# Cross-attention on one core: key and output projections as fifteen 172-column block products instead of eleven matmuls of 256 columns, with partial sums kept in PSUM

## The chip, the core and the metric

One core of one Trainium2 chip. The metric is the device time of one execution in microseconds (us). The kernel before took 1415.97 us (median of two runs, 1415.4 and 1416.54).

## What is computed

For 64 batches, all in float32; x is 64 x 256 x 512 and ctx_768 is 64 x 256 x 384, the hidden width H is 512:

```python
text_p  = einsum('bld,dh->blh', x, W_text) + b_text          # queries
audio_p = einsum('bsd,dh->bsh', ctx_768, W_audio) + b_audio  # keys and values
Q, K, V = layer_norm(text_p, g1, beta1), layer_norm(audio_p, g2, beta2), audio_p
alpha   = softmax(einsum('blh,bsh->bls', Q, K) / sqrt(512))
H_hyper = einsum('bls,bsh->blh', alpha, V) @ W_out + b_out
return layer_norm(H_hyper + x, g_out, beta_out)
```

## The kernel before

The values are never formed. The attention weights multiply the raw context rows (z, 384 wide), and z is multiplied by W_audio @ W_out, folded once at the start (`fold_multiply`, L252), with a folded bias (`bao_sb`). Every batch has five products. In float32 each `nc.tensor.matmul` call becomes two MATMUL rows and two weight loads in the profile.

- **q** (512 x 512 weights): seven block products of a Strassen-Winograd scheme, 14 calls of 256 columns; **k** (384 x 512): seven block products, 11 calls; **y**, the output (384 x 512): 11 calls. All three are `Blocks` objects: `products` (L487) fills PSUM, two products to a bank, and `leave` (L499) adds each bank to SBUF rows with VectorE, five additions of 128 x 512 per object. The sums of the left-hand blocks are made by GpSimd (`sum_x`, `sum_c`), those of the weights once at the start.
- **scores** (L526): 8 calls; **z** (`context`, L592): 6 calls, copied out of PSUM by ScalarE (L599).

So a batch is 50 calls of 256 columns. Around them: ScalarE takes the square sums (L392), scales rows (`normalise`, L420), applies gamma and beta (`affine`, L458), does the exponentials (L543), their division (L557) and the output's two statistics (L617, L622). VectorE turns 32 x 32 squares (L91, L451), takes the maxima (L536), and shifts and settles the output (L729, L738). GpSimd makes the reciprocal roots (L353, L355) and adds x to the output (`add_x`, L608). Rows that must be transposed go through DRAM: `store` writes them, `fetch` reads them back as squares, with DMAs on the SyncE queue (SP).

The order is written out by hand: each engine executes its own instructions strictly in the order in which the Python code issues them, and the tile layer inserts the semaphore waits. PSUM is six rotating one-bank buffers (`p_pj`) and two more for scores and z (`p_at`). A round of the main loop works on three batches at once: the scores of batch b, q and k of batch b+2, z and y of batch b-1. On TensorE it stands as scores, q, z, k, y, and within q, k or y no product reads what `leave` made of an earlier one: `leave` only empties banks. The one result that TensorE needs back in the same round is z, whose sums GpSimd makes for y while k runs. 62 rounds run, then the last two batches are finished in a tail.

Of the kernel before, what the change touches and what calls it, by code (L numbers as in the profile page):

```python
# [22 lines left out]
def kernel(  # L23
# [18 lines left out]

# [7 lines left out]
    scale = 1.0 / math.sqrt(H)  # L72

    const = ctx.enter_context(tc.tile_pool(name="const", bufs=1))
    xin = ctx.enter_context(tc.tile_pool(name="xin", bufs=3))
    cin = ctx.enter_context(tc.tile_pool(name="cin", bufs=3))
    blk = ctx.enter_context(tc.tile_pool(name="blk", bufs=2))
    work = ctx.enter_context(tc.tile_pool(name="work", bufs=2))
    small = ctx.enter_context(tc.tile_pool(name="small", bufs=4))
    scratch = ctx.enter_context(tc.tile_pool(name="scratch", bufs=3, space=bass.MemoryType.DRAM))  # L80
    p_pj = ctx.enter_context(tc.tile_pool(name="p_pj", bufs=6, space=PSUM))
    p_at = ctx.enter_context(tc.tile_pool(name="p_at", bufs=2, space=PSUM))

# [49 lines left out]
    def row(v, name):  # L133
        t = const.tile([P, H], F32, tag=name, name=name)
        nc.sync.dma_start(t, v.rearrange("(o h) -> o h", o=1).broadcast_to([P, H]))
        return t
# [4 lines left out]

# [4 lines left out]
    wa_sb = const.tile([P, AC, H], F32, tag="wa", name="wa")  # L146
# [14 lines left out]
    ba_sb = row(b_audio, "ba")  # L161
# [32 lines left out]
    def keep_busy(n):  # L194

        ps = p_pj.tile([P, P], F32, tag="pj", name="ps_ones")
        for _ in range(n):
            nc.tensor.matmul(ps, lhsT=ones, rhs=ones, start=True, stop=True)

    class RowTurn:  # L200

# [31 lines left out]
    def bias_parts():  # L233

        part = work.tile([P, D], F32, tag="e", name="part")
        nc.vector.tensor_scalar(part, wo_sb[:, 0, :], bac_sb[:, 0:1], None, ALU.mult)
        for k in range(1, HC):
            nc.vector.scalar_tensor_tensor(
                part, wo_sb[:, k, :], bac_sb[:, k : k + 1], part, ALU.mult, ALU.add
            )  # L240

        nc.vector.tensor_tensor(part[:1], part[:1], bo_sb, ALU.add)
        return part

    wao_sb = const.tile([P, AC, D], F32, tag="wao", name="wao")
    ps_wao = {}

    def fold_multiply(a):

        ps = ps_wao[a] = p_pj.tile([P, D], F32, tag="pj", name="ps_wao")  # L250
        for k in range(HC):
            nc.tensor.matmul(  # L252
                ps,
                lhsT=waT[k][:, bass.ts(a, P)],
                rhs=wo_sb[:, k, :],
                start=(k == 0),
                stop=(k == HC - 1),
            )

    def fold_evict(a):  # L260
        nc.scalar.copy(wao_sb[:, a, :], ps_wao.pop(a))

    def fold_bias(part):

        ps = p_pj.tile([P, D], F32, tag="pj", name="ps_bao")
        nc.tensor.matmul(ps, lhsT=ones, rhs=part, start=True, stop=True)
        bao = const.tile([P, D], F32, tag="bao", name="bao")
        nc.vector.tensor_copy(bao, ps)
        return bao
# [21 lines left out]
    H2 = H // 2  # L291

    def weight_sums(w_sb, n, name, between=lambda: None):

# [28 lines left out]
    def sum_c(cT, tag="csum"):  # L326

        part = lambda i, j: cT[:, j, bass.ts(i, P)]
        s = work.tile([P, 5, P], F32, tag=tag, name=tag)
        add = nc.gpsimd.tensor_tensor  # L330
        add(s[:, 0], part(1, 0), part(1, 1), ALU.add)
        add(s[:, 1], s[:, 0], part(0, 0), ALU.subtract)
        add(s[:, 2:4], cT[:, 0:3:2, :P], cT[:, 0:3:2, P:], ALU.subtract)
        add(s[:, 4], part(0, 1), s[:, 1], ALU.subtract)
        return {
            1: [part(0, 0)], 2: [part(0, 1), part(0, 2)], 4: [part(1, 1), part(1, 2)],
            5: [s[:, 0], part(1, 2)], 6: [s[:, 1]], 7: [s[:, 2]], 3: [s[:, 4], s[:, 3]],
        }

    def weights_of_three(w_sb, name):  # L340

        ws = weight_sums(w_sb, 1, name)
        for n, k2 in ((2, 0), (3, 1), (5, 1), (4, 0)):
            ws[n].append(w_sb[:, 2, (1 - k2) * H2 : (2 - k2) * H2])
        return ws
# [12 lines left out]
    class Projection:  # L358


        def __init__(self, name, b, srcT, w_sb, bias, nch, nt):
            self.name, self.b, self.nt, self.nch = name, b, nt, nch
            self.srcT, self.w_sb, self.bias = srcT, w_sb, bias
            self.rows = work.tile([P, nt, H], F32, tag=f"{name}r", name=f"{name}r_{b}")
# [3 lines left out]
            self.ps = {}  # L368

        def multiply(self, t, chunks):  # L370
            if t not in self.ps:
                self.ps[t] = p_pj.tile([P, H], F32, tag="pj", name=f"ps_{self.name}")
# [9 lines left out]
        def evict(self, t):  # L382
            nc.vector.tensor_tensor(self.rows[:, t, :], self.ps.pop(t), self.bias, ALU.add)
# [57 lines left out]
        def turn(self):  # L441
            self.T = work.tile(
                [P, HC, self.nt * P], F32, tag=f"{self.name}T", name=f"{self.name}T_{self.b}"
            )
            if self.name == "q" or self.b >= B - 2:
                turn(self.T, self.sq, HC)
                return


            for t in range(self.nt):  # L450
# [15 lines left out]
    class Blocks(Projection):  # L466

        def __init__(self, name, b, sides, weights, bias):
            super().__init__(name, b, None, None, bias, None, 2)
            self.sides, self.weights, self.banks = sides, weights, {}

        def products(self, *ns):

            for n in ns:  # L480
                group = next(g for g in ((1, 6), (2, 5), (3, 4), (7,)) if n in g)
                if group not in self.banks:
                    self.banks[group] = p_pj.tile([P, 2, H2], F32, tag="pj", name=f"ps_{self.name}")
                place = self.banks[group][:, group.index(n), :]
                pairs = list(zip(self.sides[n], self.weights[n]))
                for i, (side, w) in enumerate(pairs):
                    nc.tensor.matmul(  # L487
                        place, lhsT=side, rhs=w, start=(i == 0), stop=(i == len(pairs) - 1)
                    )

        def leave(self, *ns):

            bank = self.banks[(1, 6) if ns[0] in (1, 6) else ns]
            quarters = self.rows.rearrange("p t (k h) -> p (t k) h", k=2)
            c1, c2 = quarters[:, :2], quarters[:, 2:]
            add = lambda o, i0, i1: nc.vector.tensor_tensor(o, i0, i1, ALU.add)  # L499
            if len(ns) == 1:  # L500
                j = int(ns[0] == 6)
                bank = bank[:, j : j + 1, :].broadcast_to([P, 2, H2])
            if ns == (1,):
                add(c1, bank, self.bias.rearrange("p (k h) -> p k h", k=2))
            elif ns == (6,):
                add(c2, bank, c1)
            elif ns == (2, 5):
                add(quarters[:, 1:3], bank, quarters[:, 1:3])
            elif ns == (3, 4):
                add(quarters[:, 0:4:3], bank, c2)  # L510
            elif ns == (7,):
                add(c2, bank, c2)

    class Attention:
        def __init__(self, b):
            self.b, self.qT, self.kT = b, q.pop(b).T, k.pop(b).T
            self.summed = ()

        def scores(self, end=False):
            if end:  # L520
                self.sc = p_pj.tile([P, LT, S], F32, tag="pj", name="ps_sc")
            else:
                self.sc = p_at.tile([P, LT, S], F32, tag="at", name="ps_sc")
            for t in range(LT):
                for k in range(HC):
                    nc.tensor.matmul(  # L526
                        self.sc[:, t, :],
                        lhsT=self.qT[:, k, bass.ts(t, P)],
                        rhs=self.kT[:, k, :],
                        start=(k == 0),  # L530
                        stop=(k == HC - 1),
                    )
# [5 lines left out]
        def exponentials(self):  # L538

            self.e = work.tile([P, LT, S], F32, tag="e", name=f"e_{self.b}")  # L540
# [30 lines left out]
        def transpose_e(self):  # L571
            self.ps_e = p_pj.tile([P, ST, L], F32, tag="pj", name="ps_e")
# [10 lines left out]
        def context(self):  # L583

            self.zT = work.tile([P, AC, L], F32, tag="zT", name="zT")
            self.ps_z = []
            for lo in range(0, AC, 2):
                n = min(2, AC - lo)
                ps = p_at.tile([P, 2, L], F32, tag="at", name="ps_z")
                for j in range(n):  # L590
                    for s in range(ST):
                        nc.tensor.matmul(  # L592
                            ps[:, j, :],
                            lhsT=c_rows[self.b][:, s, bass.ts(lo + j, P)],
                            rhs=self.eT[:, s, :],
                            start=(s == 0),
                            stop=(s == ST - 1),
                        )
                nc.scalar.copy(self.zT[:, lo : lo + n, :], ps[:, :n, :])  # L599

        def start_products(self):

            self.o = Blocks("y", self.b, sum_c(self.zT, "zsum"), wao_blocks, bao_sb)
            self.y = self.o.rows

        def add_x(self):
            for t in range(LT):
                nc.gpsimd.tensor_tensor(self.y[:, t, :], self.y[:, t, :], x_rows[self.b][:, t, :], ALU.add)  # L608
# [22 lines left out]
        def start_output(self):  # L631
            self.y = work.tile([P, LT, H], F32, tag="yr", name=f"y_{self.b}")
# [3 lines left out]
        def multiply(self, t):  # L636
# [458 lines left out]
```

## Time and profile before

| | us |
|---|---|
| median of two runs | 1415.97 |
| span of the profiled execution, first to last instruction | 1411.8 |
| what lies outside the span, against the median | 4.2 |
| start, up to the scores of round 0 | 43.0 |
| main loop, from there to the scores of the tail | 1330.7 |
| tail | 38.1 |
| one full round (scores to scores) | 21.58 |
| busy in a full round: TensorE, VectorE, ScalarE, GpSimd | 21.58, 19.1, 14.6, 13.5 |

The profiled execution's own time is not listed apart from its span; the span is taken as that execution and 4.2 us as what lies around it. In rows of the profile, PE is TensorE's matmul, PEld its weight load, DVE VectorE, ACT ScalarE, POOL GpSimd. "x4" in a timeline means four equal rows merged, and the time beside it runs from the first one's start to the last one's end. The recorded end of a matmul is later than the start of the next: rows overlap in the pipeline, so a matmul's price is read from start to start.

### The profile page before, as it was taken

To read this page: it belongs to the slowest core of one execution; us is meant where nothing else is said; L and a number is where in the kernel's file an instruction comes from. 1 tells how busy PE (TensorE), PEld (TensorE's weight loads), DVE (VectorE), ACT (ScalarE), POOL (GpSimd) and SP (SyncE) were. 2 spreads that over 40 slices of the span, in tenths; PEclk is the share of its full clock that TensorE was granted. 3 is DMA by queue.
4 is the path that set the end of the run, shared out by engine and by line. 5 is a ranking of instruction groups with operands and counts; after the bars stand their busy time and mean duration, and the time that the engine had idled before them with its cause. 6 is when DMAs were issued, how large, how long until landed. Compare 5 with 4: busy or idle time off the path is not lost.

```text
span 1411.8 us, 22761 instructions
## 1 busy us (share of the span) xinstructions
PE 1403.2 (99%) x6437; PEld 1220.4 (86%) x6437; DVE 1230.4 (87%) x1758; ACT 935.0 (66%) x2298; POOL 871.0 (62%) x1294
## 2 busy tenths in 40 slices
PE   9999999999999999999999999999999999999998
PEld 5888888888888888888888888888888888888885
DVE  6888898898888988988988889889889888898887
ACT  4667667676676676676766766766767667667663
POOL 5556666656656666666566566666665665666645
PEclk9999999999999999999999999999999999999999
DMA  8798877888888887787887887877888888878763
GB/s 211 206 259 229 245 233 218 246 232 224 241 243 219 232 233 228 234 226 237 231 230 235 225 238 232 231 232 232 221 243 237 222 240 239 222 235 232 223 212 125
DMA packets 450437, 322.32 MB, mean 228 GB/s; under 512 B 154885, under 2 KB 382981, under 8 KB 450310
## 3 DMA queue, kind: packets, MB, share of 16 engines
q1 hardware_dynamic: 450214, 320.72, 80.3%
q8 instruction: 52, 0.85, 0.3%
q14 instruction: 75, 0.61, 0.2%
q10 hardware_dynamic: 96, 0.13, 0.0%
HBM read 203.83 MB, written 116.92 MB: 227 GB/s over the span
## 4 chain that ended last, share of the span: by engine, by line
PE 98%; DVE 1%; POOL 1%; DMA 0%; ACT 0%; issue 0%; DVEq 0%; ACTq 0%
PE ps_q L487 27%; PE ps_k L487 21%; PE ps_y L487 20%; PE ps_sc L526 15%; PE ps_z L592 12%; PE ps_wao L252 1%; PE ps_y L639 1%; PE ps_q L374 0%; PE ps_k L374 0%; DMA c<-in_ctx_dram 0%; DVE yr L499 0%; PE ps_rows L214 0%; POOL yr L608 0%; POOL x L772 0%; DVE kr L499 0%; PE ps_wa L227 0%
## 5 line engine op out<-in xcount | busy, mean ns | idle before, releaser
L499 DVE TENSOR_TENSOR qr<-ps_q,qr 128x512 f32<-128x512 f32 x252 | 174.3, 692 | 88.9 <-PE ps_q L487 86.1
L526 PE MATMUL ps_sc<-kT,qT 128*128 128x256 f32 x1024 | 231.5, 379 | 0.0
L353 POOL TENSOR_SCALAR ve<-var 128x2 f32<-128x2 f32 x126 | 43.4, 344 | 290.0 <-ACT junk L392 289.8
L526 PEld LDWEIGHTS ps_sc<-kT,qT 128*128 128x128 f32 x1024 | 194.6, 190 | 26.9 <-issue 0.5
L543 ACT ACTIVATE e<-ps_sc,nmx 128x256 f32<-128x256 f32 x128 | 59.4, 468 | 230.3 <-DVE nmx L536 230.3
L608 POOL TENSOR_TENSOR yr<-yr,x 128x512 f32<-128x512 f32 x124 | 155.7, 1277 | 70.8 <-DVE yr L499 70.8
L499 DVE TENSOR_TENSOR kr<-ps_k,kr 128x512 f32<-128x512 f32 x252 | 174.4, 692 | 22.5 <-DVE kr L499 0.9
L487 PE MATMUL ps_q<-wtsum,xsum 128*128 128x256 f32 x756 | 193.7, 379 | 0.0
L499 DVE TENSOR_TENSOR yr<-ps_y,yr 128x512 f32<-128x512 f32 x248 | 171.6, 692 | 21.7 <-DVE yr L499 0.5
L487 PE MATMUL ps_k<-wa,cT 128*128 128x256 f32 x630 | 177.1, 379 | 0.0
L592 PE MATMUL ps_z<-eT,c 128*128 128x256 f32 x768 | 176.2, 379 | 0.0
L487 PE MATMUL ps_y<-wao,zT 128*128 128x256 f32 x620 | 174.1, 379 | 0.0
L355 POOL TENSOR_TENSOR rstd<-ve,nhalf 128x2 f32<-128x2 f32 x192 | 157.3, 819 | 16.0
L592 PEld LDWEIGHTS ps_z<-eT,c 128*128 128x128 f32 x768 | 145.9, 190 | 20.3 <-issue 0.5
L487 PEld LDWEIGHTS ps_q<-wtsum,xsum 128*128 128x128 f32 x756 | 143.6, 190 | 19.5
L458 ACT ACTIVATE qT<-qT,columns 128x256 f32<-128x256 f32 x256 | 133.0, 593 | 4.1 <-DVE qT L91 4.0
L458 ACT ACTIVATE kT<-kT,columns 128x256 f32<-128x256 f32 x256 | 132.2, 588 | 2.3 <-DVE kT L91 1.3
L487 PEld LDWEIGHTS ps_k<-wa,cT 128*128 128x128 f32 x630 | 119.6, 190 | 16.2
L487 PEld LDWEIGHTS ps_y<-wao,zT 128*128 128x128 f32 x620 | 117.7, 190 | 16.0
L420 ACT ACTIVATE kr<-kr,rstd 128x512 f32<-128x512 f32 x126 | 84.0, 714 | 71.6 <-POOL rstd L355 71.6
L392 ACT ACTIVATE junk<-kr 128x512 f32<-128x512 f32 x126 | 79.4, 630 | 77.9 <-DVE kr L499 73.5
L487 PE MATMUL ps_q<-wt,xT 128*128 128x256 f32 x504 | 129.0, 379 | 0.0
(160 smaller groups left out, 2976.3 us busy)
## 6 DMA issues: line engine op xcount, KB each, us to landing
kd<-kr SPq DMA_DIRECT2D x64, 512.0 KB, 3.1
kq<-kd SPq DMA_DIRECT2D x256, 128.0 KB, 3.4
qd<-qr SPq DMA_DIRECT2D x64, 512.0 KB, 4.8
qq<-qd SPq DMA_DIRECT2D x256, 128.0 KB, 3.3
xq<-in_x_dram SPq DMA_DIRECT2D x252, 128.0 KB, 3.0
x<-in_x_dram SPq DMA_DIRECT2D x63, 512.0 KB, 4.3
out_dram<-yr SPq DMA_DIRECT2D x62, 512.0 KB, 4.8
cq<-in_ctx_dram SPq DMA_DIRECT2D x252, 96.0 KB, 2.5
```

Source lines behind the costliest of these rows:

```text
L252: nc.tensor.matmul(ps, lhsT=waT[k][:, bass.ts(a, P)], rhs=wo_sb[:, k, :], start=(k == 0), stop=(k == HC - 1),)
L353: nc.gpsimd.tensor_scalar(ve, var, EPS, None, ALU.add)
L355: nc.gpsimd.tensor_tensor(r, ve, nhalf[:, :n], ALU.pow)
L392: nc.scalar.activation(junk, self.rows[:, t, :], AF.Square, scale=1.0 / math.sqrt(H), accum_out=self.var[:, t : t + 1],)
L420: nc.scalar.mul(row, row, self.r[t])
L458: nc.scalar.activation(self.T[:, k, :], self.T[:, k, :], AF.Identity, bias=bet[:, k : k + 1], scale=gam[:, k : k + 1],)
L487: nc.tensor.matmul(place, lhsT=side, rhs=w, start=(i == 0), stop=(i == len(pairs) - 1))
L499: add = lambda o, i0, i1: nc.vector.tensor_tensor(o, i0, i1, ALU.add)
L526: nc.tensor.matmul(self.sc[:, t, :], lhsT=self.qT[:, k, bass.ts(t, P)], rhs=self.kT[:, k, :], start=(k == 0), stop=(k == HC - 1),)
L543: nc.scalar.activation(self.e[:, t, :], self.sc[:, t, :], AF.Exp, bias=self.nmx[:, t : t + 1], accum_out=self.den[:, t : t + 1],)
L592: nc.tensor.matmul(ps[:, j, :], lhsT=c_rows[self.b][:, s, bass.ts(lo + j, P)], rhs=self.eT[:, s, :], start=(s == 0), stop=(s == ST - 1),)
L608: nc.gpsimd.tensor_tensor(self.y[:, t, :], self.y[:, t, :], x_rows[self.b][:, t, :], ALU.add)
```

## The change

k (from batch 2 on; batch 1's keys become 12 plain calls) and y (batches 0 to 61) become `Thirds`: the 512 columns are padded to 516 and split into three blocks of 172 columns, the 384 inputs into three of 128, the 256 rows into two of 128. Fifteen products of 172 columns replace eleven calls of 256. The partial sums stay in one four-bank PSUM tile, `third`, that k and y use in turn: TensorE accumulates onto values that VectorE or ScalarE have written there. The products come in five groups, and between groups VectorE combines the sums:

```diff
+    third = p_all.tile([P, 4, H], F32, tag="third", name="ps_t")
+    fork = p_all.tile([P, 2, H], F32, tag="fork", name="ps_f")
...
+    class Thirds(Projection):
+        L0, M0 = third[:, 0, :W3], third[:, 0, W3 : 2 * W3]
+        T, U = third[:, 1, :W3], third[:, 1, W3 : 2 * W3]
+        L1, M1 = third[:, 2, :W3], third[:, 2, W3 : 2 * W3]
+        N0, N1 = third[:, 3, :W3], third[:, 3, W3 : 2 * W3]
...
+        def seed(self):
+            nc.scalar.copy(self.M, self.bias.rearrange("p (j h) -> p j h", j=3)[:, 0:3:2])
+        def one(self):
+            self.add_products((14, self.N0), (13, self.N1))
+        def after_one(self):
+            n1 = self.room("n1")
+            nc.vector.tensor_copy(n1, self.N1)
+            dve(self.T, self.N0, n1, ALU.subtract)
+        def two(self):
+            self.add_products((11, self.M0), (12, self.M1))
+        def three(self):
+            self.add_products((9, self.T))
+        def after_three(self):
+            t = self.room("t")
+            nc.vector.tensor_copy(t, self.T)
+            dve(self.L0, self.M0, t, ALU.add)
+            dve(self.L1, self.M1, t, ALU.subtract)
+        def four(self):
+            self.add_products((8, self.M0), (0, self.L0), (10, self.M1), (3, self.L1), (1, self.T))
+        def after_four(self):
+            m = self.room("m")
+            dve(m, self.M1, self.delta, ALU.subtract)
+            dve(self.U, self.M0, m, ALU.subtract)
+        def five(self):
+            self.add_products((6, self.N0), (5, self.N1), (2, self.M0), (4, self.M1), (7, self.U))
+        def after_five(self):
+            u, n = self.room("u"), self.room("n", 2)
+            nc.scalar.copy(u, self.U)
+            nc.scalar.copy(n, self.N)
+            dve(self.rows[:, 0, W3 : 2 * W3], self.T, u, ALU.add)
+            dve(self.ends(1), self.M, n, ALU.add)
+            d = self.room("d")
+            nc.gpsimd.tensor_tensor(d, n[:, 0], n[:, 1], ALU.subtract)
+            nc.gpsimd.tensor_tensor(self.rows[:, 1, W3 : 2 * W3], u, d, ALU.add)
+        def leave(self):
+            nc.scalar.copy(self.ends(0), self.L)
```

For y, `leave_plus` takes the place of `leave` and `add_x`: VectorE adds x to the two outer thirds on their way out of PSUM (172 and 168 columns), GpSimd to the rest. The left-hand sums are seven GpSimd additions (`third_sides`) instead of four.

q keeps its seven products and 14 calls, but as `Fork`: its sums also stay in PSUM, in the two-bank tile `fork`, seeded by ScalarE, with two ScalarE copies (`after_first`) and three VectorE additions of 256 columns (`after_six`, `after_five`) between products; `square` and `normalise` read PSUM directly.

The output of a batch comes one round later (z and y of batch b-2, statistics and store of b-3), and the parts are interleaved on TensorE. A full round of the loop now issues, with `old` = batch b-2, `last` = b-1, `settled` = b-3 (the lines for edge rounds left out, calls joined on a line where they follow each other):

```diff
+        k2.one(); k2.after_one(); k2.two()
+        old.context_two(0)
+        k2.three()
+        old.context_two(1); old.copy_two()
+        cT[b + 3] = turn_c(b + 3)
+        at.affine_keys()
+        k2.after_three()
+        old.start_products()
+        cs[b + 3] = third_sides(cT.pop(b + 3), "csum")
+        q2.six(); q2.after_six()
+        k2.four(); k2.after_four()
+        q2.five(); q2.after_five()
+        last.turn_e()
+        at.affine_queries()
+        k2.five()
+        settled.statistics()
+        k2.after_five()
+        q2.rest()
+        k2.leave()
+        old.o.seed()
+        q2.square(); q2.scales()
+        q[b + 1].turn()
+        xT[b + 3] = turn_x(b + 3)
+        at.score(0, 2)
+        old.o.one(); old.o.after_one(); old.o.two()
+        at.score(2, 3)
+        old.o.three()
+        k[b + 1].turn([0])
+        k2.square(); k2.scales()
+        old.o.after_three()
+        k[b + 1].turn([1])
+        at.score(3, 6)
+        q2.normalise(); q2.store()
+        old.o.four()
+        settled.shift(0); settled.shift(1)
+        old.o.after_four()
+        at.score(6, 8)
+        old.o.five()
+        Fork.seed()
+        k2.normalise(); k2.store()
+        q2.fetch(); k2.fetch()
+        xs[b + 3] = sum_x(xT.pop(b + 3))
+        at.maxima(); at.exponentials()
+        settled.settle(0)
+        old.o.after_five()
+        start_queries(b + 3)          # the next q's first(), after_first()
+        at.reciprocals()
+        old.o.leave_plus(x_rows[b - 2])
+        last.context_one()
+        at.divide_e()
+        k2.seed()                     # seeds the next round's keys
+        at.store_e()
+        last.copy_one()
+        settled.settle(1); settled.store()
```

Row buffers of x and context go from three to two, several others from two to one. In the tail, y of batches 60 and 61 are `Thirds` (before, only batch 61 was left over), and the last two batches stay plain.

## The prediction, as it went on record

> **What bounds the kernel now.** I read the engine totals and the chain first, then one full round by windows, then single timelines for the prices of hand-offs.
>
> ```profile
> PE 1403.2 (99%) x6437; PEld 1220.4 (86%) x6437; DVE 1230.4 (87%) x1758; ACT 935.0 (66%) x2298; POOL 871.0 (62%) x1294
> ...
> PEclk9999999999999999999999999999999999999999
> ...
> PE 98%; DVE 1%; POOL 1%; DMA 0%; ACT 0%; issue 0%; DVEq 0%; ACTq 0%
> ```
> ```profile
> 704.60:726.18 21.58, 21.58 (x101) 19.00 (x100) 19.09 (x28) 14.58 (x36) 13.51 (x21) 1.00 0.87 257
> ```
> The reader is to see that TensorE never waits in a round (21.58 of 21.58 us busy, clock 1.00), so a round is the sum of its 100 matmul rows at 216 ns. All else is hidden. A saving on TensorE counts fully, and so does any wait put into its queue.
>
> Prices per row of TensorE, by start to start: 16 score rows take 3.45 us, 216 ns at 256 columns. The 128-column transposes below stand 0.65 us per six, 108 ns. That is 0.83 ns per column, so 172 columns cost 146 ns; a call is two rows: 0.432 us at 256, 0.292 at 172.
>
> ```profile
> 704.60 3.62 PE L526 MATMUL ps_sc<-kT,qT 128*128 128x256 f32 x16
> 708.05 1.03 PE L487 MATMUL ps_q<-wt,xT 128*128 128x256 f32 x4
> ```
> ```profile
> 19.40 0.82 PE L227 MATMUL ps_wa<-ident,war 128*128 128x128 f32 x6
> 20.05 0.60 PE L487 MATMUL ps_k<-wa,cT 128*128 128x256 f32 x2
> ```
> ```profile
> L487 PEld LDWEIGHTS ps_k<-wa,cT 128*128 128x128 f32 x630 | 119.6, 190 | 16.2
> ```
> ```profile
> 11.13 0.30 PEld L374 LDWEIGHTS ps_k<-wa,cT 128*128 128x128 f32 x2
> ```
> A weight load is recorded at 190 ns, longer than 146. But two loads here take 0.30 us together, so the second began 0.11 us after the first: 190 ns is latency, not the time between loads. I take 146.
>
> [...]
>
> **Prices of hand-offs.**
>
> ```profile
> 710.64 1.03 PE L487 MATMUL ps_q<-wtsum,xsum 128*128 128x256 f32 x4
> ```
> ```profile
> 711.71 0.69 DVE L499 TENSOR_TENSOR qr<-ps_q,qr 128x512 f32<-128x512 f32 x1 [0.24 <-PE ps_q L487]
> ```
> The last of these rows ends at 711.67, VectorE starts at 711.71: a reader starts 0.20 us after TensorE's slot is over (0.16 of recorded tail, 0.04 of signal).
>
> ```profile
> 1382.09 0.45 POOL L332 TENSOR_TENSOR zsum<-zsum,zT 128x128 f32<-128x128 f32 x1
> 1382.59 0.73 PEld L487 LDWEIGHTS ps_y<-waosum,zsum 128*128 128x128 f32 x4 [0.51 <-POOL zsum L332]
> 1382.59 1.13 PE L487 MATMUL ps_y<-waosum,zsum 128*128 128x256 f32 x4
> ```
> The way back: GpSimd ends at 1382.54, the load starts 0.05 later, and four rows take 1.13 instead of 1.03: a waiting TensorE restarts 0.15 us after its releaser.
>
> ```profile
> L499 DVE TENSOR_TENSOR kr<-ps_k,kr 128x512 f32<-128x512 f32 x252 | 174.4, 692 | 22.5 <-DVE kr L499 0.9
> L268 DVE COPY bao<-ps_bao 128x512 f32<-128x512 f32 x1 | 0.7, 654 | 0.0
> L706 DVE SCALAR_TENSOR_TENSOR y<-ps_y,rden,x 128x256 f32<-128x256 f32 x2 | 1.0, 481 | 0.5 <-PE ps_y L692 0.5
> L648 DVE SCALAR_TENSOR_TENSOR y<-ps_y,rden,x 128x512 f32<-128x512 f32 x3 | 2.2, 747 | 0.6 <-PE ps_y L639 0.6
> L599 ACT COPY zT<-ps_z 128x512 f32<-128x512 f32 x64 | 36.1, 564 | 3.8 <-POOL ve L353 3.8
> L599 ACT COPY zT<-ps_z 128x256 f32<-128x256 f32 x64 | 23.8, 372 | 9.0 <-PE ps_z L592 1.5
> ```
> VectorE pays 1.04 ns per column (747 less 481, by 256). So an addition costs 0.34 us at 172 columns, 0.43 at 256, 0.52 at 344, a copy 0.30 at 172; a dependent one starts 0.03 later (0.105 where another wait stands before it, L499). ScalarE's copies, by 0.75 ns per column: 0.31 at 172, 0.44 at 344, 0.1 less where the next follows freely. No row of before has VectorE or ScalarE writing PSUM. Nearest are these rows that read it; I take their price, and as bounds 0.08 less (independent VectorE rows overlap by that much) and 0.105 more per operation.
>
> **The change, part by part.**
>
> (1) TensorE's work: k and y each go from 11 x 0.432 = 4.75 to 15 x 0.292 = 4.38. Times 124 objects that is -45.8; batch 1's keys with 12 calls add 0.4: -45.4 us. A round's rows are 28 x 0.432 + 30 x 0.292 = 20.85 us.
>
> (2) The other engines have room. VectorE: 15 additions of 512 columns (10.4 us) become 23 smaller ones (18 of `Thirds`, 3 of `Fork`, 2 with x: 8.4), so 19.1 falls to about 17. ScalarE gains three seeds, two `after_first` copies, four copies u and n and one `leave`, about 3.1: 14.6 rises to 17.7. GpSimd makes 14 additions for the sums instead of 8 (8.1 instead of 5.1, from 0.73 at 256 columns, L316, and 0.46 at 128, L331) and four more of 172 columns (0.55 each, between these), less 0.7 of `add_x`: 13.5 rises to 18. DMA moves the same bytes. None is the bound by its sum.
>
> (3) The waits. TensorE now needs VectorE's results inside the same object, and the built order of the changed kernel shows where:
>
> ```
> 209 L499 Matmult ps_t<-wa,csum 128x172 [waits Activation_49]
> 210 L499 Matmult ps_t<-wa,csum 128x172
> 211 L499 Matmult ps_t<-wa,csum 128x172 [waits DVE_49]
> ```
> Row 209 is `one` (it waits for ScalarE's seed), row 211 the first call of `two`, and its wait is for the second instruction of `after_one`, though `two` writes M and `after_one` touches N and T. The tile layer keeps the four banks of `third` in order as one tile. Between `one` and `two` TensorE has nothing else to do. All eight hand-offs of a round, walked with the prices above; zero is the start of k's `one`, times in us:
>
> - k `one` ends 0.58. VectorE copies from 0.79 to 1.09, subtracts to 1.46; `two` starts 1.60. **Stall 1.02.**
> - `two`, z, `three`, z, q's `six` run to 4.21. `after_three` starts 0.20 after `three` (2.91): three operations to 4.15, restart 4.30. **0.09.**
> - `four` to 5.76, q's `five` to 6.62. `after_four` 5.96 to 6.67. **0.20.** k's `five` 6.82 to 8.28, q's `rest` and two score calls to 11.73.
> - y's `one` waits for `old.o.seed`, behind this queue on ScalarE: z copy 3.55, gamma and beta 2 x 1.98 (L458: four in 2.08, 0.495 apart), `statistics` 2.63 (L617, L622: 712.32 to 714.95), so 10.41. Then the copies u and n to 11.06, VectorE's two additions to 11.88, `leave` to 12.36, `seed` to 12.83. Start 12.98. **1.25.**
> - y's `one` ends 13.56, but VectorE has the transposes of q and x first (2 x 1.16, to 14.19). `after_one` ends 14.87. **1.46.**
> - `two`, scores, `three`, scores run to 17.62; `after_three` ends 17.57. **0.10.** `four` and scores to 20.05; `after_four`, behind two shifts (0.64 each), ends 20.12. **0.22.**
> - y's `five` ends 21.73, q's `first` 23.46, four z calls 25.19. The next k `one` waits for `k2.seed`, on ScalarE behind the two copies of `after_first` (from 23.66) and the two divisions (to 25.15): seed to 25.59, start 25.74. **0.55.**
>
> Sum 4.89: a round takes 20.85 + 4.89 = 25.74 us instead of 21.58. GpSimd is not in this chain: its sums for y are begun at 3.9 and the first four are done before 8, and k's row parts end near 14.3, as ScalarE comes to them.
>
> (4) Ends. Rounds 0 and 1 have keys only: about 2 us each, 4. In the tail, y's `two` of batch 60 waits for `after_one`, which VectorE reaches only after maxima, statistics (2.63) on ScalarE, two shifts and two settles: from 4.9 to 12.2 us after the tail's start, 7.3; some 3 more for the other hand-offs: 10. The prologue keeps its length.
>
> **Sum:** 1411.8 - 45.4 + 60 x 4.89 (293.4) + 4 + 10 + 4.2 outside the span = **1678 us**, 1.185 of before. With 0.08 less on the 19 operations that end a stall, a round is 1.5 shorter: 1587. With 0.105 more on all 23 it is 2.4 longer: 1823.
>
> [...]
>
> **Rivals.**
> - *TensorE stays full* (the other side): if the waits are met on arrival, 1411.8 - 45.4 + 4.2 = 1371, 3.2% faster. For it: no engine is full by its sum. Against it: `two` follows `one` at once. It decides below 45.4/60 = 0.76 us of stalls a round; the two `one`-`two` gaps alone make 2.0. Chance 0.03.
> - *Only the unavoidable waits*: if ScalarE and VectorE run ahead of my walk, y's `one` doesn't wait (the chain from k's `five` is some 2.6 us under 3.45 of cover) and y's `two` waits 1.02. Stalls 3.2: 1678 - 60 x 1.69 = 1577. For it: both engines have idle time. Against it: their order is fixed, with `statistics` and the transposes ahead. 0.10.
> - *GpSimd late*: if its additions run at the 1163 and 875 ns that zsum's show beside VectorE (L333, L334) instead of 733 and 459, 14 additions take 14.0 instead of 8.1 us, k's second rows, its squares and then the exponentials come late, and y's `five` is read some 2.7 us later: a round of about 27.3, 1771. 0.12, in the range.
> - *Weight loads bind* at 190 ns: 60 rows x 0.044 = 2.6 a round, 1836. Against it the overlap above. 0.04.
>
> **The numbers.** My walk 0.69, GpSimd late 0.12, unavoidable waits 0.10, weight loads 0.04, full TensorE 0.03, stalls near break-even 0.02. The range 1575 to 1800 takes in the second rival and all but the end of the upper bound. Faster by over 2% (about what a measurement of this kernel tells from no change) 0.03, within 0.02, slower 0.95.
>
> **What would show it.** TensorE idle before the first call of `two` about 1.0 us in k and 1.5 in y, released by VectorE's subtraction; before y's `one` 1.25, released by ScalarE's seed; rounds of 25.7 us; rows of 172 columns 146 ns apart when not waiting. Wrong would be a start of `two` before `after_one` ends, a spacing near 190, or a round below 23.

## The result and the profile after

| | before | after | predicted |
|---|---|---|---|
| median, us | 1415.97 | 1824.86 (two runs: 1824.55, 1825.16) | 1678 (1575 to 1800) |
| span of the profiled execution | 1411.8 | 1822.8 | 1673.8 |
| start, up to the scores of round 0 | 43.0 | 57.7 | 43.0 |
| from there to the scores of the tail | 1330.7 | 1691.8 | 1582.7 |
| tail | 38.1 | 73.3 | 48.1 |
| one full round | 21.58 | 27.31 | 25.74 |

The changed kernel takes 1.288 times the time of the one before (95% interval 1.284 to 1.292). The direction and the main mechanism were as predicted, the size was not: 149 us of the span are missing from the sum, 109 in the loop, 15 at the start, 25 in the tail. The time lies 25 us above the range.

The page of the changed kernel, busy time by engine, the clock in 40 slices and the chain that ended last:

```profile
PE 1572.8 (86%) x7419; PEld 1314.6 (72%) x7419; DVE 1077.5 (59%) x2248; ACT 1143.7 (63%) x2929; POOL 1139.2 (62%) x1946
...
PEclk9899999999999999999999999999999999999988
...
PE 54%; ACT 26%; DVE 8%; DMA 6%; issue 3%; POOL 1%; SPq 1%; DVEq 0%; ACTq 0%; POOLq 0%
```

No engine is full any more, and the chain of work now runs through ScalarE and VectorE for a third of the span: by the spacing of its rows TensorE's own work fell to 20.85 us a round, and waiting took its place. (Its recorded busy time rose, from 1403.2 to 1572.8 us, since it counts rows at half clock, four in 1.52 us, and the recorded tails of rows ahead of a wait, four in 0.85 us where the spacing gives 0.58.)

From one round on TensorE, `one` of the keys to the next (timeline; L499 is the line that issues the products of `Thirds`):

```profile
819.91 0.85 PE L499 MATMUL ps_t<-wa,csum 128*128 128x172 f32 x4 [0.33 <-ACT ps_t L509]
821.64 0.85 PE L499 MATMUL ps_t<-wa,csum 128*128 128x172 f32 x4 [0.88 <-DVE ps_t L480]
...
827.63 1.04 PE L499 MATMUL ps_t<-wa_thirds,cT 128*128 128x172 f32 x6
...
831.09 1.03 PE L650 MATMUL ps_sc<-kT,qT 128*128 128x256 f32 x4
833.06 0.82 PE L499 MATMUL ps_t<-wao,zsum 128*128 128x172 f32 x4 [0.95 <-POOL ve L366]
834.94 1.52 PE L499 MATMUL ps_t<-wao,zsum 128*128 128x172 f32 x4 [1.05 <-DVE ps_t L480]
```
```profile
832.51 0.45 ACT L509 COPY ps_t<-bao 128x344 f32<-128x344 f32 x1
```

The second fence is ScalarE's. Read from start to start with 0.146 us per row of 172 columns and 0.216 per row of 256 (four score rows from 831.09 end at 831.96, `one` starts at 833.06), TensorE stands 0.49 us ahead of k's `one` (walked: 0.55), 1.15 ahead of `two` (1.02), 1.10 ahead of y's `one` (1.25), 1.30 ahead of y's `two` (1.46). The releasers are those of the walk, with one correction to the profile's own word: y's `one` at 833.06 is put down to GpSimd, but ScalarE's seed (L509) ends at 832.96, 0.10 before; that row ended last. All waits of the round come to 4.7 us, 4.89 walked. What the walk doesn't have is the 1.52 us of the last row, where four rows took 0.85 elsewhere. Two stretches of it by windows (length, busy PE, PEld, DVE, ACT, POOL, granted clock, DMA share, GB/s):

```profile
831.54:834.95 3.41, 1.41 (x8) 0.78 (x6) 3.38 (x7) 2.88 (x9) 3.00 (x8) 1.00 0.32 57
834.95:838.37 3.42, 3.42 (x10) 3.15 (x11) 0.96 (x3) 3.14 (x7) 3.26 (x6) 0.50 0.16 61
```

In the stretch that holds both stalls of y TensorE was busy for 1.41 of 3.41 us; in the next one its clock was 0.50, and there the four rows took those 1.52 us. Half of 3.41, 1.7 us, is my estimate of what that costs. The clock's records have 67 such stretches, all of one or a few times 3.413 us. In the loop's full rounds there are 58. They lie 8 x 3.413 = 27.31 us apart, with one gap of 16: that is the length of a round. In the gap lies the one full round without a half clock, and it took 26.74 us (shown below, with `fill`).

The tail and the start have waits of their own (timelines):

```profile
44.63 2.07 PE L585 MATMUL ps_f<-wt,xT 128*128 128x256 f32 x4 [4.87 <-ACT ps_f L581]
...
64.53 1.49 PE L499 MATMUL ps_t<-wa,csum 128*128 128x172 f32 x4 [3.18 <-ACT ps_t L509]
```
```profile
1763.53 1.52 PE L499 MATMUL ps_t<-wao,zsum 128*128 128x172 f32 x4 [8.04 <-DVE ps_t L480]
...
1809.52 5.34 PE L831 MATMUL ps_t<-wao,zT 128*128 128x256 f32 x12 [9.49 <-DVE y L787]
```

The first two are seeds that ScalarE copies late, at the start and in round 0; round 1 has two more such waits, 4.37 and 2.05 us. The wait of 8.04 is the one that I had at 7.3. The wait of 9.49 I had missed: the last product writes banks 1 and 2 of `third`, and it waits until VectorE has emptied bank 0, since the four banks are kept in order as one tile. (In the one-bank kernel below, the same product starts at 1532.03, right behind six rows of 0.43 us that start at 1529.37.) Half-clock stretches lie there too: up to 100 us TensorE was busy for 22.9 us under half clock, in the tail for 11.7. By the same estimate half of these, 11.5 and 5.9 us, is the most that they can have cost.

### The profile page after: what moved, and what is told of

Its sections match the earlier page's. It is cut to its first block, busy times and chain, and to the rows that moved or that the text cites. A ratio compares the mean times of both kernels' runs of the same rounds, so it can differ in the third digit from the quotient of the medians.

```text
span 1822.8 us, 25850 instructions
## 1 busy us (share of the span) xinstructions
PE 1572.8 (86%) x7419; PEld 1314.6 (72%) x7419; DVE 1077.5 (59%) x2248; ACT 1143.7 (63%) x2929; POOL 1139.2 (62%) x1946
## 4 chain that ended last, share of the span: by engine, by line
PE 54%; ACT 26%; DVE 8%; DMA 6%; issue 3%; POOL 1%; SPq 1%; DVEq 0%; ACTq 0%; POOLq 0%
PE ps_t L499 28%; PE ps_f L585 11%; PE ps_sc L650 11%; ACT junk L620 4%; ACT qT L471 3%; ACT kT L471 3%; PE ps_z L716 3%; ACT e L681 3%; ACT ps_t L509 3%; DVE ps_t L480 2%; DMA c<-in_ctx_dram 2%; DVE n L531 2%; ACT junk L756 2%; DVE kr L480 2%; ACT junk L761 2%
## 5 line engine op out<-in xcount | busy, mean ns | idle before, releaser
L499 PE MATMUL ps_t<-wao,zsum 128*128 128x172 f32 x496 | 141.7, 424 | 128.1 <-DVE ps_t L480 71.7
L311 POOL TENSOR_TENSOR zsum<-zT 128x256 f32<-128x256 f32 x124 | 73.3, 591 | 242.8 <-ACT zT L734 231.5
L499 PEld LDWEIGHTS ps_t<-wao,zsum 128*128 128x128 f32 x496 | 101.0, 251 | 166.4 <-DVE ps_t L480 87.9
L585 PE MATMUL ps_f<-wtsum,xsum 128*128 128x256 f32 x756 | 197.0, 384 | 1.0 <-ACT s L596 0.6
L499 PE MATMUL ps_t<-wao_thirds,zsum 128*128 128x172 f32 x744 | 184.9, 347 | 2.5 <-DVE ps_t L480 2.5
L499 PE MATMUL ps_t<-wa,csum 128*128 128x172 f32 x496 | 107.5, 340 | 79.6 <-DVE ps_t L480 54.4
L499 PE MATMUL ps_t<-wa_thirds,csum 128*128 128x172 f32 x744 | 173.1, 328 | 0.0
L499 PEld LDWEIGHTS ps_t<-wao_thirds,zsum 128*128 128x128 f32 x744 | 142.1, 213 | 39.1 <-DVE ps_t L480 24.5
L499 PEld LDWEIGHTS ps_t<-wa,csum 128*128 128x128 f32 x496 | 74.6, 193 | 121.0 <-DVE ps_t L480 70.8
L585 PEld LDWEIGHTS ps_f<-wtsum,xsum 128*128 128x128 f32 x756 | 143.1, 193 | 19.2 <-ACT s L596 0.9
L499 PEld LDWEIGHTS ps_t<-wa_thirds,csum 128*128 128x128 f32 x744 | 121.6, 191 | 42.7 <-DVE ps_t L480 39.5
L370 POOL TENSOR_TENSOR rstd<-ve,nhalf 128x2 f32<-128x2 f32 (+1 forms) x192 | 136.1, 709 | 16.0
L585 PE MATMUL ps_f<-wt,xT 128*128 128x256 f32 x504 | 132.5, 386 | 10.2 <-ACT ps_f L581 10.2
L480 DVE TENSOR_TENSOR kr<-ps_t,u 128x172 f32<-128x172 f32 x62 | 20.9, 337 | 190.9 <-ACT n L548 114.4
```

What stands on the lines that cost most here:

```text
L311: less = lambda o, i0, i1: nc.gpsimd.tensor_tensor(o, i0, i1, ALU.subtract)
L370: nc.gpsimd.tensor_tensor(r, ve, nhalf[:, :n], ALU.pow)
L480: nc.vector.tensor_tensor(o, i0, i1, op)
L499: nc.tensor.matmul(place, lhsT=self.sides[n], rhs=self.weights[n], start=(n == 14), stop=True, skip_group_check=True,)
L585: nc.tensor.matmul(place, lhsT=side, rhs=w, start=False, stop=True, skip_group_check=True)
```

## The experiments

Theory: the walked waits, most of which come from `third` being one tile and from what stands ahead in ScalarE's and VectorE's queues, and on top of them the half clock, set off by the two stalls of y. Rival: the clock, or the time as a whole, follows something else (narrow rows, an engine's total work). Times are medians; the ratios are to the kernel before on the same chip (1413.4 to 1415.9). The diffs leave out `if` lines for the edge rounds.

**Filled stalls.** A `fill` issues two calls of 256 columns into a bank that nobody reads any more:

```diff
+            old.fill(2)
             old.o.one()
+            old.fill(2)
             old.o.after_one()
```


> The changed kernel with four extra matmul calls of 256 columns in each round with a y: two ahead of y's `one` and two between `one` and `two`, into a PSUM bank whose content nobody reads any more. That is 60 x 4 x 0.43 = 104 us of added TensorE work, of which each pair (0.86 us) lies inside a stall (1.2 and 1.29 us), so the order of all else stays. Theory (the half clock comes from two short stalls that fall into one stretch of 3.4 us): the half-clock stretch of 3.4 us a round is gone, a round is 20.85 + 4.8 = 25.7 us instead of 27.3, and the time falls by about 60 x 1.64 = 98 us to 1727. Rival (the half clock has another cause, such as the narrow rows or the sum of work on all engines): the clock's pattern stays and the time is 1825 or more, since work is added.

Measured 1789.3 us, ratio 1.266 (1.264 to 1.268). 104 us of work added, 35 us less time, and the clock of the span 0.986 instead of 0.931, with no half-clock stretch in the full rounds: here the half clock went with TensorE's idle time. But 98 less were expected. The rest is in `five` (timeline of TensorE, then of VectorE, this kernel; then VectorE in the changed kernel):

```profile
818.75 0.85 PE L499 MATMUL ps_t<-wao,zsum 128*128 128x172 f32 x4 [0.19 <-DVE ps_t L480]
...
824.96 0.85 PE L499 MATMUL ps_t<-wao_thirds,zsum 128*128 128x172 f32 x4 [0.86 <-DVE ps_t L480]
```
```profile
822.00 2.28 DVE L874 SCALAR_TENSOR_TENSOR yr<-yr,nm,go 128x512 f32<-128x512 f32 x2
824.21 0.32 DVE L480 TENSOR_TENSOR m<-ps_t,bao_delta 128x172 f32<-128x172 f32 x1
```
```profile
812.16 1.37 DVE L868 SCALAR_TENSOR_TENSOR yr<-yr,nm,go 128x512 f32<-128x512 f32 x2
```

The two shifts ahead of `after_four` take 2.28 instead of 1.37 us, and they now run beside the last of GpSimd's sums of x (822.56 to 823.74), which takes 1.18 instead of 0.73. With the half clock TensorE was late enough for them not to meet: in the changed kernel that sum ends at 812.12, and the shifts start at 812.16. The changed kernel shows the same with nothing added, in its one full round without a half clock (window; TensorE at `five`; VectorE; GpSimd):

```profile
683.74:710.48 26.74, 22.68 (x116) 18.93 (x116) 17.36 (x35) 17.97 (x47) 17.73 (x31) 1.00 0.79 187
```
```profile
704.98 0.85 PE L499 MATMUL ps_t<-wao_thirds,zsum 128*128 128x172 f32 x4 [0.85 <-DVE ps_t L480]
```
```profile
702.01 2.28 DVE L868 SCALAR_TENSOR_TENSOR yr<-yr,nm,go 128x512 f32<-128x512 f32 x2
```
```profile
702.57 1.18 POOL L299 TENSOR_TENSOR xsum<-xT,xsum 128x256 f32<-128x256 f32 x1
```

So part of the half clock's cost stood in for another wait: net it is 27.31 - 26.74 = 0.57 us a round, some 33 us in 58 rounds, close to the 35 that came back.

**Filled stalls, shifts later**, and **that move alone**:

```diff
-            settled.shift(0)
-            settled.shift(1)
         if old:
             old.o.after_four()
...
         at.maxima()
+            settled.shift(0)
+            settled.shift(1)
```

> The kernel with the filled stalls (extra calls ahead of y's `one` and between `one` and `two`), and the two shifts of the settled batch moved behind `after_four` and the maxima on VectorE. In the filled kernel TensorE waited 1.01 us ahead of y's `five` (0.2 in my walk), because the two shifts ahead of `after_four` took 2.28 us beside GpSimd's sums of x, not 1.37. Theory (the time that the clock gave back was taken by that wait): `five` waits 0.2 again, a round is 26.74 - 0.8 = 25.9 us and the time 1789 - 60 x 0.8 = 1741, about the 1727 expected of the fill alone. Rival (the shifts' work has to be done somewhere and moves the wait to the exponentials): 1780 or more.

> The changed kernel with only that move of the two shifts, and nothing filled. Theory: with the half clock in place VectorE's work lies elsewhere against GpSimd's (the shifts took 1.37 us, `five` waited 0.2), so there is nothing to gain: 1825 within 10. Rival (the shifts cost 0.8 us a round in the changed kernel too): 1777.

Measured 1735.0 (ratio 1.226, 1.224 to 1.228) and 1816.3 (1.283, 1.281 to 1.285), both as the theory has it. With the fill a round is 25.83 us: 20.9 of rows, 1.7 of fill, 3.2 of waits. Without it the half clock stays and the move gives 9 us, about 4 of them in three rounds that ran free at 25.8. The clock's net cost together with the late shifts is thus 1825 - 1735 = 90 us, and without the second move only 35.

**One call instead of four**, ahead of y's `one`:

> The changed kernel with one extra call of 256 columns a round (0.43 us) ahead of y's `one`, where it waited 1.1; the wait of 1.29 ahead of `two` is left as it is. So the two stalls of y hold 0.7 + 1.3 = 2.0 us without work instead of 2.4, within 3.4. Theory (the half clock depends on the share of a stretch of 3.4 us without work, and kernels with up to 1.7 us had none, this one with 2.4 had it): the point lies between these; a mean clock of 0.93 and 1825 if it lies below 2.0, a clock of 0.985 and about 1790 if above. Rival (the single longest stall of 1.29 us sets it off): 0.93 and 1825 too, so only a clock of 0.985 tells the two apart.

Measured 1789.9, ratio 1.265 (1.263 to 1.267), clock 0.984. The longest stall stood as it was (1.05 in the profile's own count), so a single stall is not what sets it off. By windows, one of the stretches with the least work in it and the one behind it:

```profile
681.97:685.38 3.41, 1.83 (x9) 1.15 (x9) 3.38 (x6) 3.04 (x9) 3.00 (x8) 1.00 0.24 40
685.38:688.79 3.41, 3.41 (x19) 2.96 (x20) 2.28 (x6) 3.12 (x7) 3.25 (x6) 1.00 0.22 83
```

1.83 of 3.41 us busy, and the clock stays at 1.00. Over some 300 stretches of each kernel, laid on the grid of 3.413 us of its clock records, the changed kernel's 40 stretches ahead of a half clock were busy for 0.41 to 0.44, all its others at full clock for 0.69 or more; in this one none was below 0.54 and none was followed by a half clock. Two stretches outside these windows come closer, one ahead of the changed kernel's missing half clock, one ahead of the only half clock in this kernel's full rounds:

```profile
694.99:698.40 3.41, 1.78 (x9) 1.09 (x7) 3.29 (x6) 2.50 (x7) 3.11 (x7) 1.00 0.68 112
```
```profile
146.08:149.49 3.41, 1.63 (x8) 0.97 (x6) 3.38 (x6) 2.70 (x9) 2.98 (x8) 1.00 0.58 100
149.49:152.90 3.41, 3.24 (x10) 2.98 (x11) 0.98 (x3) 3.38 (x7) 3.04 (x6) 0.50 0.21 79
```

After 0.52 the clock stayed, after 0.48 it fell. In a later kernel (`ordered`) it fell after 0.50 and not after 0.45, so in these kernels the point lies near one half and is not sharp by this count.

**Statistics later** on ScalarE, and **`two` ahead of `after_one`** (the second also for the keys and only for the loop):

```diff
-            settled.statistics()
         k2.after_five()
         q2.rest()
         k2.leave()
             old.o.seed()
+            settled.statistics()
```
```diff
             old.o.one()
+            old.o.two()
             old.o.after_one()
-            old.o.two()
```

> The changed kernel with the statistics of the settled batch moved behind k's `leave` and y's seed on ScalarE (2.63 us that no longer lie ahead of the seed); nothing else is moved. By the walk y's `one` no longer waits (1.2 us a round) and y's `two` waits 0.4 less, so 1.6 us a round. Theory with the shared stretch: with one y stall of about 1 us left the half clock goes too, another 1.64 us; a round is about 24.1 us and the time 1825 - 60 x 3.25 = 1630. Rival (the half clock is not tied to those two stalls): only the 1.6 us go, 1729. Second rival (what is gained there is lost at another wait, q's square being 2.6 us later on ScalarE): 1800 or more.

> The changed kernel with the two calls of `two` written ahead of `after_one`, for k and y; they touch other columns, so the sums are the same. The built order then has `two` free of the wait and `three` waiting for VectorE's subtraction. Theory (the stall comes from the order in which the whole tile is kept, and the walk of the hand-offs is right): k's stall of 1.15 falls to about 0 since `two` (0.58) and a call of z (0.43) cover the 1.0, y's falls from 1.29 to about 0.4; about 2.0 us a round, and with the y stalls 0.9 us shorter in their stretch the half clock goes as well: a round near 23.7 and a time near 1610. Without that second part: 1705. Rival (TensorE would wait for VectorE in any order, the time being VectorE's): 1800 or more.

Measured 1683.5 (ratio 1.191, 1.189 to 1.193) and 1721.9 (1.219, 1.217 to 1.221). In both the half clock is gone from the full rounds. In the first y's `one` starts at once, yet a round is 24.94, not 24.1: `five` waits 0.57 for the shifts (0.11 before), and y's `two` still waits 1.04, not 0.9. That is 0.6 of the 0.9 us missing; the rest I didn't follow. The second shows where I was wrong about one tile (VectorE, then TensorE):

```profile
822.27 0.34 DVE L531 COPY n<-ps_t 128x172 f32<-128x172 f32 x1 [2.33 <-PE ps_t L499]
```
```profile
820.73 1.43 PE L499 MATMUL ps_t<-wa,csum 128*128 128x172 f32 x8 [0.33 <-ACT ps_t L509]
...
823.04 0.56 PE L499 MATMUL ps_t<-wa_thirds,csum 128*128 128x172 f32 x2 [0.45 <-DVE ps_t L480]
```

`two` follows `one` without a gap, but VectorE's copy of `one`'s result starts only after `two` has ended: the order of one tile binds in both directions. k's wait is halved (1.15 to 0.61), not gone; y's is 0.70, and `five` waits 0.87 for the shifts as in `fill`. So a round is 25.63 instead of 23.7: its waits still come to 4.8 us, and the gain is the half clock's alone.

**One-bank tiles**: `third` as four tiles, the operations that spanned two banks as two each.

```diff
-    third = p_all.tile([P, 4, H], F32, tag="third", name="ps_t")
+    t0, t1, t2, t3 = [
+        p_all.tile([P, H], F32, tag=f"third{n}", name=f"ps_t{n}x") for n in range(4)
+    ]
```


> The changed kernel with the four-bank tile as four tiles of one bank, and with the few operations that spanned two banks (seed, `leave`, the last addition of ends) as two of 172 columns each; the order is unchanged. The built waits are then by bank: y's and k's `one` no longer wait for the seed, `two` waits for the seed only, `three` for `after_one`, half of `five` for nothing. Theory: stalls of about 2.5 us a round are left (y `two` 0.8 for the seed behind the statistics, y `three` 0.9 behind VectorE's transposes, 0.8 for the rest) instead of 4.8, and the half clock goes: a round near 23.4, time near 1590; 1690 if the half clock stays. Rival (not the tile's order but the arrival of VectorE's and ScalarE's results sets the time): within 2% of 1825.

Measured 1548.7, ratio 1.095 (1.093 to 1.098): 276 us less from this alone, with the same arithmetic in the same order. A round is 23.06. Keys have no wait left; y has two (timeline):

```profile
805.24 0.53 PE L502 MATMUL ps_t1x<-wao_thirds,zsum 128*128 128x172 f32 x2 [1.15 <-DVE ps_t1x L483]
...
810.17 0.56 PE L502 MATMUL ps_t0x<-wao_thirds,zT 128*128 128x172 f32 x2 [0.20 <-DVE ps_t1x L483]
```

**Can fifteen products win?** Four more kernels on top of the one-bank tiles, all with the shifts behind the maxima. `ordered` has the statistics behind y's seed, and

```diff
             last.turn_e()
...
+        q[b + 1].turn()
+            xT[b + 3] = turn_x(b + 3)
         k2.after_five()
```

> The kernel with one-bank tiles, and on top of it the order changed at three places: the transposes of q and x ahead of k's `after_five` on VectorE (where it waited 3.2 us for ScalarE), the statistics behind y's seed on ScalarE, and the shifts behind the maxima. The three stalls left in a round of the one-bank kernel (0.21 for the seed, 1.31 for `after_one` behind the transposes, 0.37 for `after_four` behind the shifts) each lose what stands ahead of them. Theory: a round of 20.85 us of rows and some 0.5 us of restarts and rests, 21.3 instead of 23.06; 1549 - 60 x 1.76 = 1443. Below that it can't come to 1416, since start and end together are some 45 us longer than before. Rival (another engine's chain, such as GpSimd's sums of zT or the way of the exponentials, becomes the limit): a round stays above 22, 1485 or more.

Measured 1707.5, ratio 1.207 (1.205 to 1.208), a miss: rounds of 23.5 to 27.7 us, and the half clock back in 22 of the 330 stretches from 299 to 1487 us. VectorE's queue shows why:

```profile
827.48 0.71 DVE L78 STREAM_TRANSPOSE eT<-eq 128x512 f32<-128x512 f32 x1 [2.77 <-DMA eq<-ed]
828.11 1.20 DVE L78 STREAM_TRANSPOSE qT<-qq 128x1024 f32<-128x1024 f32 x1
829.24 1.20 DVE L78 STREAM_TRANSPOSE xT<-xq 128x1024 f32<-128x1024 f32 x1
830.37 0.30 DVE L483 TENSOR_TENSOR kr<-ps_t1x,u 128x172 f32<-128x172 f32 x1
```

What I had moved ahead stood behind a transfer that wasn't back. So `ordered3` takes it away from there and has the statistics at the start of the round; `edges` changes start and tail as well (shown: the moves named in what was expected):

```diff
         k2.two()
+            settled.statistics()
...
-            last.turn_e()
+        q[b + 1].turn()
+            xT[b + 3] = turn_x(b + 3)
...
         k[b + 1].turn([1])
+            last.turn_e()
```
```diff
-    load_x_rows(B - 3)
     load_c_rows(B - 3)
+    last.fetch_e()
+    load_x_rows(B - 3)
...
     at.score(0, 8)
-    last.turn_e()
+    old.o.one()
+    old.o.after_one()
+    old.o.two()
     at.maxima()
```

> The kernel with one-bank tiles and another order at four places: on VectorE the transposes of q and x ahead of k's `after_five` and the transposes of e no longer ahead of them but behind k's last transposes (in the kernel `ordered` everything on VectorE stood behind the transposes of e, which waited up to 2.8 us for e to come back from DRAM); the shifts behind the maxima; on ScalarE the statistics at the start of the round, where ScalarE waited 3.3 us for z. Theory (`ordered` failed by that one DMA wait at the head of VectorE's queue, and by q's square being late behind the statistics): the stalls of 1.31 and 0.37 go, and the seed is in time; a round of 20.85 us of rows plus about 0.4, 21.2; 1549 - 60 x 1.85 = 1438. Rival (a chain through GpSimd or ScalarE sets the round): above 22, 1485 or more.

> The same, with start and end in another order: the constants of the queries' seed and that seed ahead of the columns, and the keys' first seed ahead of q's squares (waits of 4.15 and 2.53 us in the one-bank kernel); in the tail the audio rows are fetched ahead of e, y's three steps of batch 60 run right behind the scores, and the statistics, shifts and settles behind them (waits of 4.98 and 3.62). Expected: some 5 us less at the start and 8 to 10 less at the end, 1424; with a round of 21.0 or less it would pass the kernel before at 1415. If start and end are bound by other chains (GpSimd's weight sums, ScalarE's affine rows), within 5 us of the kernel without these moves.

Measured 1489.9 (ratio 1.053, 1.051 to 1.054) and 1485.4 (1.049, 1.047 to 1.051). A round is 22.13 in both. The moves at start and end gave 4.5 us, where 13 to 15 were expected: the case named for other chains that bind there. One wait of a size is left in the round (timeline and window of `edges`):

```profile
819.90 1.13 PE L591 MATMUL ps_f<-wtsum,xsum 128*128 128x256 f32 x4 [0.84 <-POOL xsum L301]
```
```profile
819.90:842.03 22.13, 21.29 (x117) 19.14 (x117) 17.37 (x38) 18.02 (x50) 18.84 (x31) 1.00 0.91 226
```

GpSimd, which I had ruled out as the bound, is the next in line: busy for 18.84 of 22.13 us in this window (what was expected of `final` has 19.9), and not free to spread it. `final` changes its queue (not shown: one addition of x goes to VectorE):

```diff
             old.start_products()
+            settled.statistics_end()
-            cs[b + 3] = third_sides(cT.pop(b + 3), "csum")
...
             xs[b + 3] = sum_x(xT.pop(b + 3))
+            cs[b + 3] = third_sides(cT.pop(b + 3), "csum", rest=rest)
...
             old.o.leave_plus(x_rows[b - 2])
+            rest.pop()()
```

> The kernel `edges` with less and other work in GpSimd's queue. There a round was 22.13 us with one stall left, 1.0 us of q's second product for GpSimd's sums of x (GpSimd was busy for 19.9 of 22.1 us, and stood 2.25 us ahead of the sums of zT for the statistics). Moved: the reciprocal roots of the statistics behind the sums of zT, the sums of c behind those of x (their last two behind the sums into y), and one addition of x to VectorE. Theory (GpSimd's queue is now what TensorE waits for): the 1.0 us goes, a round of 21.2, 1485 - 60 x 0.9 = 1430. Rival (GpSimd's work as such, some 20 us a round beside VectorE, is the limit): 22 us a round, 1475 or more. Neither gets below the kernel before at 1415: start and end hold some 35 us more than before, against 45 us that the narrow products save in all.

Measured 1516.3, ratio 1.071 (1.070 to 1.073): the rival. A round is 22.45, since the wait moved to the sums of c (0.96 us ahead of k's `three`). Of the 31 us that it lost against `edges` 60 such rounds make 19; the other 12 I didn't follow further. No version came below the kernel before. The best, `edges`, is 70 us above it: against the 1371 of a full TensorE it loses 60 x (22.13 - 20.85) = 77 us in the loop's rounds and some 37 elsewhere.

## Why the prediction was right or wrong

- **That TensorE bound the kernel, and a wait put into its queue counts fully:** right. Rows of 172 columns are 0.146 us apart (six rows from 827.63 in 1.04 us, tail of 0.16 included), so the narrower products save what was said. The rival of the weight loads would have given 1836, close to the measured time; it is wrong all the same, since the spacing of the rows excludes it.
- **The hand-offs:** right, 4.7 us a round against 4.89, each within 0.2, with the releasers named, as long as the half clock was there. The prices of VectorE and ScalarE writing PSUM held: 0.34 for an addition of 172 columns, 0.45 for the seed of 344. That four banks in one tile caused the wait of `two` is shown by the one-bank kernel.
- **The clock, the step that failed in the loop:** the walk prices each stall by itself and at full clock, and the sum has no term for rows at half clock. The half-clock stretches are 3.413 us long, on a fixed grid, and those of the full rounds follow a stretch in which TensorE was busy for 0.31 to 0.46, nearly all for 0.41 to 0.44: two gaps of 1.1 and 1.3 us that fall into one stretch were enough here. With 1.7 us a round, 25.74 becomes 27.4, against 27.31. That would have given about 1780.
- **The shifts at 0.64 each:** hidden by the first miss. Beside GpSimd two of them take 2.28 us, and `five` would have waited 0.8 longer at full clock. So neither the clock alone nor the walk alone was right; taking the clock away gave 35 us, with the shifts moved 90. Where the shifts and GpSimd's sum meet, both are slower in the trace (2.28 us instead of 1.37, 1.18 instead of 0.73); why, no run shows.
- **Rounds 0 and 1 at 4 us, "the prologue keeps its length", the tail at 10:** too small, by about 15, 15 and 25 us. I walked one wait of the tail (7.3, measured 8.04) and put 3 us to all others; the wait of 9.49 on bank 0 is the same whole-tile order that I had named for the loop, not looked for in the tail. At the start and in rounds 0 and 1 I didn't walk the seeds at all (waits of 4.87, 3.18, 4.37 and 2.05). The half clock can by the estimate above have cost up to 5.9 there and 11.5 ahead of 100 us. How these 55 us divide exactly, no run shows.
- **The other rivals:** TensorE neither stayed full nor met only the unavoidable waits, since y's `one` did wait for the seed behind the statistics (1.10). GpSimd was in time in the changed kernel; it is late once the other waits are gone. That the round of 27.3 in that rival is the one measured is chance: `five` of y was not read late, and the half clock made up the length.

## What to carry to other kernels

Sum TensorE's idle time over stretches as long as those of the clock's records, 3.413 us here, not stall by stall: in the changed kernel two waits of 1.1 and 1.3 us a round fell together, TensorE was busy for 0.31 to 0.46 of that stretch, and the next one ran at a clock of 0.50. For sums that go back and forth between TensorE and another engine in PSUM, try tiles of one bank: the four-bank tile was ordered as a whole, in both directions, and one-bank tiles took 276 us off (1824.9 to 1548.7). Ahead of any move in the queue of an engine, ask what now stands in front of it, and whether that is a transfer: in `ordered` VectorE stood 2.77 us behind one, and with it all that was issued behind.

## What the runs showed of the hardware

- The changed kernel's round was as long as eight stretches of its clock's grid: 27.31 us is 8 x 3.413. The one round without the half clock took 26.74. With the moved shifts three rounds ran free at 25.83 to 25.85 us, and behind them the rounds were 27.36 and the half clock was back. What holds a round to the grid, no run tests.
- Added work shortened the program: one call of 0.43 us a round that does nothing took 35 us off (1824.9 to 1789.9).
